# A fused attention and mixture-of-experts layer on one core: the first chunk's front worked in halves of two token tiles

## The chip, the core and the metric

The kernel runs on one core of a Trainium2 chip. The metric is device time in microseconds (us). The engines are TensorE (PE in the profile, its weight loads PEld), VectorE (DVE), ScalarE (ACT), GpSimd (POOL) and SyncE (SP), which issues most DMAs. The kernel before took 575.56 us, the median of three runs (575.51 to 577.62).

## The reference

`x` holds 4096 tokens (2 x 2048) of 256 features. It is normalised (`xn`), and three things are added: `x` itself, an attention branch and a feed-forward branch, both fed by `xn`.

```python
xn = (x - mean(x)) / sqrt(var(x) + eps)
# attention: 16 heads of 16; q, k, v = xn @ W_in.T
xq, xk = clip(q / 4, -1, 1), clip(k / 4, -1, 1)
Tq, Tk = cheb(xq), cheb(xk)                    # Chebyshev polynomials
num = (Tq * cumsum(Tk * v) * beta).sum(orders) # prefix sums over the tokens
den = (Tq.sum(-1) * cumsum(Tk.sum(-1)) * beta).sum(orders)
attn = (num / (den + eps)) @ W_out.T
# feed-forward: a second layernorm, one routed expert of 8, one shared
xf = layernorm(xn) * ln_w + ln_b
top = argmax(xf @ router_w); w = sigmoid(max(xf @ router_w))
routed = (silu(w*xf @ gate[top]) * (w*xf @ up[top])) @ down[top]
shared = (silu(xf @ sh_gate) * (xf @ sh_up)) @ sh_down
out = x + attn + xn + routed + shared
```

Everything is float32.

## The kernel before

The tokens are cut into 8 chunks of 512, and a chunk into NT = 4 tiles of 128 tokens. A bank is one of six 128x512 places for products.

**Front of a chunk** (`stat` L415, `roots` L425, `front` L467). For each tile DVE computes mean and variance (L420, L421). For all tiles of a group (chunk 0 alone, chunk 1 alone, then 2 and 3, then 4 to 7) `roots` adds epsilon (L432, L433), ACT takes square roots (L435), DVE inverts and refines them (L440 to L444) and forms the bias and scale columns `nm` (L449 to L451). `front` normalises the tiles to `z` (L479 on DVE, L483 on ACT), PE transposes them by feature half `k`, four tiles into one bank (L504), and each bank is evicted with `ln_w` and `ln_b` into the transposed operand `xfT` (L507 on ACT, L509 on DVE). In chunk 0 `k` = 0 is evicted by ACT and `k` = 1 by DVE; the statistics of all later chunks wait for chunk 0's DVE eviction (`evicted`). Chunk 0 also gets its attention operand by PE: ACT writes `xn` for each tile (L496), PE transposes it (L524), the copies go to `xnT` (L526, L527). Later chunks get `xnT` by a row of ratios that goes through memory (L461 to L471, L517). L562 turns X into the sum's start, x + xn. `z`, and for later chunks `xnT` and `xfT`, are spilled to memory by SP (L528, L567, L572).

**The rest.** Router logits (L540, L548); `route` (L634) sorts the tokens by expert and makes tables of slots (PE at L699, L700, L817); `shared` (L840) multiplies `xfT` by the gate and up weights in four column blocks `f` (L849, products `pg` and `pu`), takes silu on ACT (L855), multiplies on DVE (L857) and applies the down weights (L866, added to X at L882, for the very last tiles in two steps at L873); `attend` (L888) does the attention of a chunk, whose products start at L911; `expert` (L1081) takes a tile of slots: gather (L1107), transposes (L1115), gate and up (L1125), silu and product (L1131, L1133), transposes (L1138, L1140, L1141), down (L1146), copy (L1149, L1150), scatter to `y_dram` (L1153). At the end `y_dram`, the routed result, is read chunk by chunk (L1175) once all scatters have landed, added to X (L1184) and X is stored (L1188).

**What sets the order.** Each step is recorded as an operation with an engine, a planned cost, what it reads and writes, the buffers it takes and a priority (`op`, L113). `Plan.order` (L156) then walks through planned time: whenever an engine is free, it takes the ready operation of the lowest priority number whose buffers are to be had. What comes out is a fixed order of instructions for each engine; at run time an engine runs its own in that order and waits on semaphores. So a change of one operation's cost, priority or needs can alter the order of the whole program. `shared` products have the highest numbers (`SHA` = 50 and up), so PE takes them where nothing else is ready.

Of the kernel before, what the change touches and what calls it, by code (L numbers as in the profile page):

```python
# [20 lines left out]
P = 128  # L21
# [233 lines left out]
def kernel(  # L255
# [158 lines left out]

    def stat(c):  # L415
        for t in range(NT):
            i = c * NT + t

            def f(c=c, t=t, i=i):
                V.bn_stats(stats[:, i, :], X[c][:, t, :])  # L420
                V.bn_aggr(mv[:, i, :], stats[:, i, :])  # L421

            op("DVE", 0.58, f, r=[("X", c, t)], w=[("mv", i)], prio=FRONT + 0.1 * c - 0.15, after=evicted)

    def roots(cs):  # L425
        a, b = cs[0] * NT, (cs[-1] + 1) * NT
        n = slice(a, b)
        keys = [("mv", i) for i in range(a, b)]
        p = FRONT + 0.1 * cs[0] + 0.01

        def f():
            V.tensor_scalar(ve[:, 0, n], mv[:, n, 1], EPS, None, ALU.add)  # L432
            V.tensor_scalar(ve[:, 1, n], mv[:, n, 1], 1.0 + EPS, EPS * EPS, ALU.mult, ALU.add)  # L433
        op("DVE", 0.35, f, r=keys, w=[("ve", a)], prio=p)
        op("ACT", 0.21, lambda: A.activation(rs[:, :, n], ve[:, :, n], AF.Sqrt),  # L435
           r=[("ve", a)], w=[("rs", a)], prio=p, table="sqrt")

        def h():
            r_, u_, v_ = rs[:, :, n], nu[:, :, n], ve[:, :, n]
            V.reciprocal(r_, r_)  # L440

            V.tensor_tensor(u_, r_, r_, ALU.mult)
            V.scalar_tensor_tensor(u_, u_, -0.5, v_, ALU.mult, ALU.mult)
            V.scalar_tensor_tensor(r_, u_, 1.5, r_, ALU.add, ALU.mult)  # L444
        op("DVE", 0.8, h, r=[("ve", a), ("rs", a)], w=[("r", a // NT + k) for k in range(len(cs))], prio=p)

        def h():

            V.scalar_tensor_tensor(nm[:, 0, n], mv[:, n, 0], -1.0, rs[:, 0, n], ALU.mult, ALU.mult)  # L449
            begun.append(V.tensor_scalar(nm[:, 1, n], rs[:, 0, n], 1.0, None, ALU.add).ins)  # L450
            V.scalar_tensor_tensor(nm[:, 2, n], mv[:, n, 0], -1.0, rs[:, 1, n], ALU.mult, ALU.mult)  # L451

            if a:
                V.tensor_tensor(ratio[:, n], rs[:, 1, n], ve[:, 1, n], ALU.mult)
                V.tensor_tensor(ratio[:, n], ratio[:, n], rs[:, 0, n], ALU.mult)
        op("DVE", 0.8, h, r=[("ve", a)] + [("r", c) for c in cs] + keys,
           w=[("nm", c) for c in cs] + [("ratio", a)], prio=p + 0.015)
        if a:

            pr, row = Buf(bank_p, f"pr_{a}"), Buf(ratio_p, f"row_{a}")  # L460
            op("PE", MT, lambda: T_.transpose(pr.t[: b - a, :P], ratio[:, n], ident), r=[("ratio", a)], w=[pr],  # L461
               alloc=[pr, row], prio=p - 0.5)
            op("ACT", 0.25, lambda: A.copy(row.t[: b - a, :P], pr.t[: b - a, :P]), r=[pr], w=[row], prio=p - 0.5)
            op("POOL", 1.0, lambda: G.dma_start(out=ratio_dram[a:b], in_=row.t[: b - a, :P]),
               r=[row], w=[("ratio_dram", c) for c in cs], nbytes=8 * KiB, prio=p)

    def front(c):  # L467
# [7 lines left out]
        for t in range(NT):  # L475
            i = c * NT + t

            def f(t=t, i=i):
                V.tensor_scalar(zall[:, i, :], X[c][:, t, :], mv[:, i, 0:1], rs[:, 1, i : i + 1],  # L479
                                ALU.subtract, ALU.mult)  # L480

            def f_(t=t, i=i):
                A.activation(zall[:, i, :], X[c][:, t, :], AF.Identity,  # L483
                             bias=nm[:, 2, i : i + 1], scale=rs[:, 1, i : i + 1])
            if c:
                op("ACT", 0.59, f_, r=[("X", c, t), ("r", c), ("nm", c)], w=[("z", i)], prio=p, alt=[("DVE", 0.36, f)])
            else:
                op("DVE", 0.36, f, r=[("X", c, t), ("r", c)], w=[("z", i)], prio=p)
        xnT, xfT = Buf(xnT_p, f"xnT_{c}"), Buf(xfT_p, f"xfT_{c}")
        v2 = lambda b: b.t.rearrange("p (k t) -> p k t", k=KD)  # L490
        if c == 0:

            xn2 = [Buf(ratio_p, f"xn_{i}") for i in range(2)]
            v4 = lambda t: xn2[t // 2].t[:, ts(t % 2, D)]
            for t in range(NT):
                op("ACT", 0.59, lambda t=t: A.activation(  # L496
                    v4(t), X[0][:, t, :], AF.Identity, bias=nm[:, 0, t : t + 1], scale=rs[:, 0, t : t + 1]),
                   r=[("X", 0, t), ("nm", 0)], w=[(xn2[t // 2], t)], prio=p, alloc=[xn2[t // 2]] if t % 2 == 0 else [])
        for k in range(KD):
            bk = Buf(bank_p, f"tr_{c}_{k}")  # L500

            def f(bk=bk, k=k):
                for t in range(NT):
                    T_.transpose(bk.t[:, ts(t, P)], zall[:, c * NT + t, ts(k, P)], ident)  # L504
            op("PE", 4 * MT, f, r=[("z", c * NT + t) for t in range(NT)] + ([rows] if c else []), w=[bk],
               alloc=[bk, xfT, xnT] if k == 0 else [bk], prio=p)
            on = [("ACT", 0.77, lambda bk=bk, k=k: A.activation(  # L507
                v2(xfT)[:, k, :], bk.t, AF.Identity, bias=lnb[:, k : k + 1], scale=lnw[:, k : k + 1])),
                  ("DVE", 0.69, lambda bk=bk, k=k: V.tensor_scalar(  # L509
                v2(xfT)[:, k, :], bk.t, lnw[:, k : k + 1], lnb[:, k : k + 1], ALU.mult, ALU.add))]  # L510

            o = op(*on[k if c == 0 else 0], r=[bk, "ln"], w=[(xfT, k)],
               prio=p if c else -2.0, alt=on[1:] if c else [])
            if c == 0:
                evicted[:] = [o]
            if c:
                op("DVE", 0.69, lambda bk=bk, k=k: V.tensor_tensor(v2(xnT)[:, k, :], bk.t, rows.t, ALU.mult),  # L517
                   r=[bk, rows], w=[(xnT, k)], prio=p)
        for k in range(KD if c == 0 else 0):
# [10 lines left out]
           r=[("z", c * NT + t) for t in range(NT)], w=[("z_dram", c)], nbytes=512 * KiB, prio=p)  # L530
        fronts.append(xfT)
        if c % 2:
# [4 lines left out]
            def f():  # L537
                for k in range(KD):
                    for i in range(2):
                        T_.matmul(pl.t[ts(i * KD + k, QD), :], rw[:, k, :], v2(pair[i])[:, k, :],  # L540
                                  start=True, stop=True)
            op("PE", 1.0, f, r=[(b, k) for b in pair for k in range(KD)] + ["rw"], w=[pl], alloc=[pl], prio=p)
            lgT = Buf(tv_p, f"lgT_{c}")
# [15 lines left out]
        for t in range(NT):  # L559
            i = c * NT + t  # L560
            kw = dict(bias=nm[:, 0, i : i + 1], scale=nm[:, 1, i : i + 1])
            op("ACT", 0.59, lambda t=t, kw=kw: A.activation(X[c][:, t, :], X[c][:, t, :], AF.Identity, **kw),  # L562
               r=[("nm", c), (xfT, 0)], w=[("X", c, t)], prio=ROUTE + 1.0)
        if c < STAY:
            xfTs[c] = xfT
        else:
            op("SP", 0.45, lambda: S_.dma_start(out=xf_dram[c], in_=v2(xfT)),  # L567
               r=[(xfT, 0), (xfT, 1)], w=[("xf_dram", c)], nbytes=512 * KiB, prio=p)
        if c == 0:
# [5 lines left out]
    for cs in ([0], [1], [2, 3], [4, 5, 6, 7]):  # L575
        for c in cs:
            stat(c)
        roots(cs)
        for c in cs:
# [50 lines left out]

    op("POOL", 6.5, constants, r=[("nm", 0)], w=["constants"], prio=FRONT)


    def route():  # L634
# [36 lines left out]
        def f():  # L671
# [4 lines left out]
            V.tensor_scalar(edge, iota[:, : NJ + 1], float(P), None, ALU.mult)  # L676
        op("DVE", 0.8, f, r=["iota_i"], w=["iota", "tok1"] + ones_hot + whats, alloc=ones_hot + whats, prio=FRONT + 0.75)
        op("DVE", 0.42, lambda: V.tensor_reduce(top, logits, AX.X, ALU.max),
# [155 lines left out]
    def load_T(kind, c, pool, src, prio, gate):  # L834
        b = Buf(pool, f"{kind}_{c}")
        op("SP", 0.45, lambda: S_.dma_start(out=b.t.rearrange("p (k t) -> p k t", k=KD), in_=src[c]),
           r=[(f"{kind}_dram", c)], w=[(b, 0), (b, 1)], alloc=[b], nbytes=512 * KiB, prio=prio, after=gate)
        return b

    def shared(c, gate):  # L840
# [3 lines left out]
        for f in range(KF):  # L844
            pg, pu, h = Buf(bank_p, f"pg_{c}_{f}"), Buf(bank_p, f"pu_{c}_{f}"), Buf(hT_p, f"hT_{c}_{f}")

            def mm(b, wt, f=f):
                for k in range(KD):
                    T_.matmul(b.t, wt[:, k, ts(f, P)], vx(k), start=(k == 0), stop=(k == KD - 1))  # L849
            o = op("PE", 2 * MM, lambda mm=mm, pg=pg: mm(pg, sg), r=[(xfT, 0), (xfT, 1), "sg"], w=[pg],  # L850
                   alloc=[pg, pu, h], prio=SHA + c)
            first = first or o
            op("PE", 2 * MM, lambda mm=mm, pu=pu: mm(pu, su), r=[(xfT, 0), (xfT, 1), "su", pg], w=[pu],
               prio=SHA + c - 0.1)
            op("ACT", 0.62, lambda h=h, pg=pg: A.activation(h.t, pg.t, AF.Silu), r=[pg], w=[h], prio=SHQ,  # L855
               table="silu")
            op("DVE", 0.69, lambda h=h, pu=pu: V.tensor_tensor(h.t, h.t, pu.t, ALU.mult), r=[pu, h], w=[h],  # L857
               prio=SHQ)
            hT.append(h)
# [371 lines left out]
```

## Time and profile before

| | |
|---|---|
| median of 3 runs | 575.56 us (575.51, 575.56, 577.62) |
| the profiled execution | 576.52 us, of which the span from first to last instruction is 574.5 |
| first instruction of PE | 7.85 us after the span's start |
| end of PE's last product | 570.80 |
| DVE busy, 100 to 200, 200 to 300, 300 to 400, 400 to 500 | 94.3, 94.2, 93.0, 91.8 us |
| bytes moved by DMA | 132.67 MB, mean 231 GB/s |

In the timeline a row gives the start, the length, engine, line, operation, what is written and read, and a count where equal instructions are merged; a bracket says how long the engine was idle before and what ended that. A float32 product or transpose that the program has once can appear as two records (512 columns), or as one (a transpose). Matmuls overlap, so the time of one in a row of many is the distance between starts, not the length of a record.

### The profile page before, as it was taken

How to read it: one execution, taken by the hardware profiler on the slowest of the kernel's cores; microseconds unless marked ns; L12 is line 12 of the kernel's file. 1: busy time of each engine (PE TensorE's matmuls, PEld its weight loads, DVE VectorE, ACT ScalarE, POOL GpSimd, SP SyncE). 2: the span in 40 equal slices, each digit the busy share in tenths (PEclk: the TensorE clock that was granted, in tenths of full speed). 3: DMA queues.
4: the chain of work that ended last, by engine and by line, in shares of the span. 5: the costliest groups of instructions: out<-in, count | busy, mean ns of one | idle time of the engine just before them, and what ended most of it. 6: DMA issues, size and time to landing. Idle time of an engine off the chain costs nothing.

```text
span 574.5 us, 8088 instructions
## 1 busy us (share of the span) xinstructions
PE 562.9 (98%) x2651; PEld 303.7 (53%) x2651; DVE 485.0 (84%) x787; ACT 240.4 (42%) x471; POOL 95.1 (17%) x113
## 2 busy tenths in 40 slices
PE   4999999999999999999999999999999999999997
PEld 2456564765554644564664545545454555653565
DVE  5989999998999999899999999999998999721353
ACT  5679973014532553363355445435442632221100
POOL 4111000022033011203212030221222112010100
PEclk9999999999999999999999999999999999999999
DMA  8857660644369739817994995799398679950395
GB/s 283 269 163 254 224 254 2 240 159 134 110 222 376 233 91 352 289 65 218 317 342 154 294 317 207 238 373 373 93 323 277 201 243 371 375 199 10 102 309 183
DMA packets 87689, 132.67 MB, mean 231 GB/s; under 512 B 5681, under 2 KB 52063, under 8 KB 87648
## 3 DMA queue, kind: packets, MB, share of 16 engines
q1 hardware_dynamic: 83152, 121.65, 63.1%
q0 software_dynamic: 3952, 10.51, 5.4%
q8 instruction: 21, 0.34, 0.3%
q14 instruction: 20, 0.16, 0.1%
q10 hardware_dynamic: 544, 0.00, 0.1%
HBM read 113.26 MB, written 19.15 MB: 230 GB/s over the span
## 4 chain that ended last, share of the span: by engine, by line
PE 98%; DVE 1%; DMA 0%; issue 0%; DVEq 0%
PE bank L1125 22%; PE bank L849 20%; PE bank L911 15%; PE bank L1146 11%; PE bank L866 10%; PE bank L1049 5%; PE bank L1138 3%; PE psk L941 3%; PE psq L941 2%; PE bank L504 1%; PE bank L1115 1%; PE bank L817 1%; PE psk L954 1%; PE psk L1035 1%; PE bank L540 1%; PE bank L1022 0%
## 5 line engine op out<-in xcount | busy, mean ns | idle before, releaser
L1125 PE MATMUL bank<-big,wide 128*32 128x512 f32 (+1 forms) x360 | 106.2, 596 | 0.0
L1153 POOL DMA_INDIRECT y_dram<-wide,give_i x33 | 41.9, 1270 | 308.7 <-ACT wide L1149 140.1
L911 PE MATMUL bank<-xnT,w_in 128*128 128x512 f32 x192 | 86.3, 595 | 0.0
L978 DVE TENSOR_TENSOR_SCAN tv<-ones,carry,tv 128x512 f32<-128x512 f32 x60 | 76.7, 1278 | 1.1
L849 PE MATMUL bank<-xfT,sg 128*128 128x512 f32 x128 | 62.8, 614 | 0.0
L1125 PEld LDWEIGHTS bank<-big,wide 128*32 128x32 f32 (+1 forms) x360 | 37.1, 147 | 46.5 <-issue 42.5
L849 PE MATMUL bank<-xfT,su 128*128 128x512 f32 x128 | 60.6, 595 | 0.0
L866 PE MATMUL bank<-sd,hT 128*128 128x256 f32 x256 | 57.5, 380 | 0.0
L911 PEld LDWEIGHTS bank<-xnT,w_in 128*128 128x128 f32 x192 | 35.7, 190 | 39.1 <-issue 36.5
L855 ACT ACTIVATE hT<-bank 128x512 f32<-128x512 f32 x32 | 19.1, 597 | 84.5 <-PE bank L849 83.5
L866 PEld LDWEIGHTS bank<-sd,hT 128*128 128x128 f32 x256 | 48.0, 190 | 10.0 <-issue 3.5
L1107 POOL DMA_INDIRECT wide<-z_dram,take_i x33 | 37.6, 1141 | 84.9 <-DVE give_i L828 68.4
L1146 PE MATMUL bank<-big,wide 128*32 128x256 f32 (+1 forms) x312 | 48.5, 384 | 0.0
L998 DVE TENSOR_TENSOR o<-o,tv 128x512 f32<-128x512 f32 x64 | 44.4, 694 | 1.8
L1131 ACT ACTIVATE wide<-bank,slot_s 128x512 f32<-128x512 f32 x33 | 22.7, 687 | 50.0 <-PE bank L1125 50.0
L1146 PEld LDWEIGHTS bank<-big,wide 128*32 128x32 f32 (+1 forms) x312 | 32.0, 144 | 18.7 <-issue 10.1
L849 PEld LDWEIGHTS bank<-xfT,sg 128*128 128x128 f32 x128 | 23.5, 194 | 29.0 <-issue 26.8
L933 DVE SCALAR_TENSOR_TENSOR T<-T 128x1024 f32<-128x1024 f32 x32 | 38.0, 1215 | 0.0
L849 PEld LDWEIGHTS bank<-xfT,su 128*128 128x128 f32 x128 | 23.5, 190 | 26.4 <-issue 25.5
L1133 DVE SCALAR_TENSOR_TENSOR wide<-bank,slot_s,wide 128x512 f32<-128x512 f32 x33 | 24.7, 747 | 13.6 <-PE bank L1125 12.4
L857 DVE TENSOR_TENSOR hT<-hT,bank 128x512 f32<-128x512 f32 x32 | 21.8, 682 | 16.3 <-PE bank L849 15.8
L919 ACT ACTIVATE T<-bank 128x512 f32<-128x512 f32 x32 | 19.1, 597 | 39.4 <-PE bank L911 39.4
(206 smaller groups left out, 884.2 us busy)
## 6 DMA issues: line engine op xcount, KB each, us to landing
big<-in_gate_w SPq DMA_DIRECT2D x46, 512.0 KB, 6.0
big<-in_up_w SPq DMA_DIRECT2D x44, 512.0 KB, 4.8
big<-in_down_w SPq DMA_DIRECT2D x39, 512.0 KB, 7.4
xfT<-in_down_w SPq DMA_DIRECT2D x15, 512.0 KB, 7.3
xfT<-in_up_w SPq DMA_DIRECT2D x9, 512.0 KB
z_dram<-big SPq DMA_DIRECT2D x8, 512.0 KB, 6.3
xfT<-in_gate_w SPq DMA_DIRECT2D x8, 512.0 KB, 5.7
X<-in_x SPq DMA_DIRECT2D x7, 512.0 KB
```

The lines of the kernel that those rows point to most:

```text
L849: T_.matmul(b.t, wt[:, k, ts(f, P)], vx(k), start=(k == 0), stop=(k == KD - 1))
L866: T_.matmul(po.t[:, ts(i, D)], hT[f].t[:, ts(tp * 2 + i, P)], sd[:, f, :], start=(f == 0), stop=(f == KF - 1))
L911: T_.matmul(pm.t, w_in[:, k, ds(i * D + g * P, P)], xnT.t[:, ts(k, CH)], start=(k == 0), stop=(k == KD - 1))
L933: op("DVE", 1.27, lambda i=i, j=j, q=part: V.scalar_tensor_tensor(q[i](), q[j](), off[i], q[1](), ALU.subtract, ALU.mult), r=[(T, j)] + X2 ...
L941: T_.matmul(pt.t[ts(i - 1, QD), :], heads[:, 24 - g * HB : 24 - g * HB + QD], half[i](side), start=(g == 0), stop=(g == KD - 1 and (i > KD ...
L978: o_ = op("DVE", 1.25, lambda b=b, i=i, g=g: V.tensor_tensor_scan(b.t, ones[:, 0:1].to_broadcast([P, CH]), b.t, 0.0 if opening else old[:, ...
L998: op("DVE", 0.66, lambda o=o, b=b: V.tensor_tensor(o(), o(), b.t, ALU.add), r=[b, ok], w=[ok], prio=p)
L1049: T_.matmul(pa.t[:, ts(i, D)], o2.t[:, ds(g * CH + (tp * 2 + i) * P, P)], w_out[:, g, :], start=(g == 0), stop=(g == KD - 1))
L1107: op("POOL", 1.28, lambda: G.indirect_dma_start(out=zt.t, out_offset=None, in_=z_dram, in_offset=bass.IndirectOffsetOnAxis(ap=take_i[:, j ...
L1125: T_.matmul(b.t[n, :], xT.t[:, ds(k * P + n.start, n.stop - n.start)], wt.t[:, ts(k, FF)], start=(k == 0), stop=(k == KD - 1), skip_group_ ...
L1146: T_.matmul(py.t[n, :D], hmT.t[:, ds(i * P + n.start, n.stop - n.start)], wd.t[:, ts(i, D)], start=(i == 0), stop=(i == KF - 1), skip_grou ...
L1153: y_ins.append(G.indirect_dma_start(out=y_dram, out_offset=bass.IndirectOffsetOnAxis(ap=give_i[:, j : j + 1], axis=0), in_=yt.t, in_offset ...
```

## The change

Chunk 0 goes through the front in two halves of two tiles.

- **Statistics and roots.** The first three tiles' statistics come first; the fourth tile's wait for the first half's inverse roots. `roots` runs for tiles 0 and 1, then for tiles 2 and 3. The columns `nm` are split off into `means`, which for chunk 0 runs once for all four tiles and waits for the first half's DVE eviction.
- **Transposes and evictions.** A bank now holds both feature halves of two tiles. Each half is evicted by two instructions of 128x256, `k` = 0 on ACT and `k` = 1 on DVE.
- **Products.** For `f` = 0 and 1 of chunk 0 gate and up products are issued by halves of 256 columns with priorities of their own (-5, -4.5, -4, -3.5); silu and the DVE product follow once for both halves.
- **Waits.** The casts of `route` (L672 to L676) and the statistics of later chunks wait for the last half's DVE eviction. GpSimd's `constants` (L584) waits for `nm` as before. Evictions of later chunks get the priority -2.0.

```diff
+    HT = NT // 2
+    def part(c, t):
+        return (0, t // HT) if c == 0 else (c, 0)
+    def xf_keys(c, b, h=None):
+        return [(b, k, n) for k in range(KD) for n in ((0, 1) if c == 0 else (0,)) if h in (None, n)]
...
-        op("DVE", 0.8, h, r=[("ve", a), ("rs", a)], w=[("r", a // NT + k) for k in range(len(cs))], prio=p)
+        scaled = op("DVE", 0.8, h, r=[("ve", a), ("rs", a)], w=[("r", k) for k in parts], prio=p)
+        return parts, p, scaled
+    def means(a, b, parts, p, behind=()):
...
+        for h in range(2 if c == 0 else 0):
+            bk = Buf(bank_p, f"tr_{c}_{h}")
+            hs = slice(h * HT * P, (h + 1) * HT * P)
+            for t in range(h * HT, (h + 1) * HT):
+                def f(bk=bk, h=h, t=t):
+                    for k in range(KD):
+                        T_.transpose(bk.t[:, ds((k * HT + t - h * HT) * P, P)], zall[:, t, ts(k, P)], ident)
+                op("PE", 2 * MT, f, r=[("z", t)], w=[(bk, t)],
+                   alloc=[] if t % HT else [bk, xfT, xnT] if h == 0 else [bk], prio=-6.0)
...
+            op("ACT", 0.46, lambda src=src, hs=hs: A.activation(
+                v2(xfT)[:, 0, hs], src(0), AF.Identity, bias=lnb[:, 0:1], scale=lnw[:, 0:1]),
+               r=keys, w=[(xfT, 0, h)], prio=-2.0)
+            o = op("DVE", 0.42, lambda src=src, hs=hs: V.tensor_scalar(
+                v2(xfT)[:, 1, hs], src(1), lnw[:, 1:2], lnb[:, 1:2], ALU.mult, ALU.add),
+               r=keys, w=[(xfT, 1, h)], prio=-2.0)
+            if h == 0:
+                means(0, NT, [(0, 0), (0, 1)], FRONT, [o])
+            evicted[:] = [o]
...
+        if cs == [0]:
+            stat(0, range(HT + 1))
+            stat(0, range(HT + 1, NT), [roots(0, HT)[2]])
+            roots(HT, NT)
...
-        op("DVE", 0.8, f, r=["iota_i"], w=["iota", "tok1"] + ones_hot + whats, alloc=ones_hot + whats, prio=FRONT + 0.75)
+        op("DVE", 0.8, f, r=["iota_i"], w=["iota", "tok1"] + ones_hot + whats, alloc=ones_hot + whats, prio=FRONT + 0.75, after=evicted)
...
+            halves = (0, 1) if c == 0 and f < 2 else (None,)
+            for n in halves:
+                def mm(b, wt, f=f, n=n):
+                    cols = slice(0, CH) if n is None else slice(n * CH // 2, (n + 1) * CH // 2)
+                    for k in range(KD):
+                        T_.matmul(b.t[:, cols], wt[:, k, ts(f, P)], vx(k)[:, cols], start=(k == 0), stop=(k == KD - 1))
+                cost, q = (2 * MM, SHA + c) if n is None else (2 * M256, -5 + n)
+                o = op("PE", cost, lambda mm=mm, pg=pg: mm(pg, sg), r=xf_keys(c, xfT, n) + ["sg"], w=[(pg, n)],
+                       alloc=[] if n else [pg, pu, h], prio=q)
+                first = first or o
+                op("PE", cost, lambda mm=mm, pu=pu: mm(pu, su), r=xf_keys(c, xfT, n) + ["su", (pg, n)], w=[(pu, n)],
+                   prio=q - 0.1 if n is None else q + 0.5)
```

## The prediction

> **What bounds the kernel now.** I read the page's busy shares and its chain of waits first, then what TensorE waited for, then the timelines of the first 36 us and of the last 45.
>
> ```profile
> PE 562.9 (98%) x2651; PEld 303.7 (53%) x2651; DVE 485.0 (84%) x787; ACT 240.4 (42%) x471; POOL 95.1 (17%) x113
> ...
> PE 98%; DVE 1%; DMA 0%; issue 0%; DVEq 0%
> ...
> PE bank L504 <- DVE big L479: 7.9, 1, 7.9
> ```
>
> TensorE (PE) carries the chain, and its list of waits has one entry: 7.9 us before its first instruction. From then on it is never short of work. So the time is the sum of three parts: what lies ahead of dense PE work, the PE work itself (which the order hardly alters), and what lies behind its last product. The change acts on the first part; the planner, which orders the whole program anew, may act on the last.
>
> The front, from the timelines:
>
> ```profile
> 5.66 0.17 DVE L432 TENSOR_SCALAR ve<-mv 128x4 f32<-128x4 f32 x1
> ...
> 5.93 0.21 ACT L435 ACTIVATE rs<-ve 128x8 f32<-128x8 f32 x1 [2.61 <-DVE ve L433]
> ...
> 6.46 0.20 DVE L440 RECIPROCAL rs<-rs 128x8 f32<-128x8 f32 x1
> ...
> 7.29 1.38 DVE L479 TENSOR_SCALAR big<-X,mv,rs 128x256 f32<-128x256 f32 x4
> ...
> 9.29 0.76 ACT L507 ACTIVATE xfT<-bank,lnb,lnw 128x512 f32<-128x512 f32 x1
> ```
> ```profile
> 7.85 2.20 PE L504 MATMUL bank<-ident,big 128*128 128x128 f32 x8 [7.85 <-DVE big L479]
> 10.10 3.78 PE L849 MATMUL bank<-xfT,sg 128*128 128x512 f32 x4
> 13.68 1.29 PE L524 MATMUL bank<-ident,wide 128*128 128x128 f32 x8
> 14.80 1.88 PE L849 MATMUL bank<-xfT,su 128*128 128x512 f32 x4
> ```
>
> The reader is to see two things. PE's first product waits for the eviction that ends at 10.05. And the four records from 10.10 take 3.58 us to the next instruction, those from 14.80 only 1.72 (the next starts at 16.52): 0.85 us against 0.43 apiece. PE runs at half rate until about 14.2, where the pitch of the L524 transposes halves; the PEclk column says 1.00 all the same.
>
> The end:
>
> ```profile
> 536.33 0.98 POOL L1153 DMA_INDIRECT y_dram<-wide,give_i  x1 [1.87 <-DMA y_dram<-wide,give_i]
> ...
> 538.96 0.92 SPq L1175 DMA_DIRECT2D xnT<-y_dram  x2
> ...
> 567.38 0.69 DVE L882 TENSOR_TENSOR X<-X,bank 128x512 f32<-128x512 f32 x1 [1.44 <-PE bank L866]
> 568.11 1.22 DVE L1184 TENSOR_TENSOR X<-X,xfT 128x1024 f32<-128x1024 f32 x1
> 570.84 0.75 DVE L873 TENSOR_TENSOR X<-X,bank 128x256 f32<-128x256 f32 x2 [1.51 <-PE bank L866]
> ```
>
> PE ends at 570.80. The whole add of the routed result (L1184) is done before; only two 128x256 adds and their stores follow. The span ends at 574.47, 3.67 us behind PE.
>
> **The front, step by step.** Two tiles' statistics need two pairs at a pitch of 0.53 (the pairs start at 3.39, 3.95, 4.48): the second aggregate starts at 4.38, the added epsilon 0.22 later as in before (5.44 to 5.66), Sqrt at 4.87 (0.20 behind the second of them). The third tile's pair fills VectorE (DVE) until 5.27; Reciprocal stands there, the first normalised tile 0.83 later (6.46 to 7.29) at 6.10, the second at 6.43, the first transpose 0.56 behind the first (7.29 to 7.85): 6.66. The half's last transpose starts near 7.3 and ends near 7.7. ScalarE (ACT) must run the second half's Sqrt first, which its queue holds ahead of the eviction: the fourth tile's pair starts at 6.76, so Sqrt runs 7.68 to 7.89. The 128x256 eviction isn't in the trace; between 0.46 (L1118, 128x128) and 0.77 (L507, 128x512) I take 0.56: it ends at 8.40, and the first product starts at 8.45 instead of 10.10, 1.65 us sooner.
>
> From there nothing leaves PE idle: two gate ops of four 256-column records (1.71 each at half rate) last to 11.9, the second half's transposes, whose tiles are normalised by 9.8, to 12.8, and two up ops on the first half cover the second half's evictions, done near 13.5. Moved work: the means, the casts and the next statistics stand later on DVE, under those ops; the xn copies start near 9.9 and are done near 15, PE transposes them near 19. SyncE's (SP) loads keep their order: gate and up weights are issued at 2.69 and 3.17, and at the 300 GB/s of the first 20 us the 1.05 MB up to the gate weights are in by about 7; the cover is 1 us, and a later landing would shift the first product one for one.
>
> Work done by 14.2, in full-rate time, with a transpose at 0.109 (eight from 33.91 to 34.78): before, eight transposes (0.87) and half of the 3.9 us since 10.10 (1.96), together 2.83; after, four transposes (0.44) and half of the 5.7 us since 8.45 (2.87, the other four among it), together 3.31. Gain **0.47**, if full rate comes at the same time. If it moves forward by the same 1.65, half of that more: **1.30**. One trace can't tell what sets the moment of full rate, so both ends: 4.1 us later (the dense stretch ahead of it, 10.1 to 14.2) turns the 0.47 into a loss of 1.6, as much sooner into a gain of 2.5. I take 0.9, between the two readings.
>
> [...]
>
> **PE work.** Sixteen 512-column records become 32 of 256: 0.216 each (3.46 us for 16, L866) against 0.429 (5.15 for 12, L911), +0.05. In the built order PE changes between full and quarter-array products 131 times instead of 128; a change costs 0.09 (0.52 against 0.43 ahead of L941): +0.28. Elsewhere products that wait for an ACT or DVE step stand at least 1.1 us of PE work behind its source, against 1.0 before: no new stall, at 0; bounds 0 and 3, a few such waits of under a microsecond each behind a DVE that is 92 to 94% busy from 100 to 500.
>
> **The tail.** Six of chunk 0's eight gate and up ops now stand before the first attention product, instead of three, and everything from there on stands later in PE's order. Behind the last expert's product the built order holds 8 gate/up ops and 32 down products, 13.7 + 13.8 = 27.5 us; in before it is 36.3 (534.5 to 570.8). The scatter, and with it the loading of the routed result, comes 8 us nearer to PE's end: first load about 24 us before it, not 31.8.
>
> On DVE the closing rows are now: the add of X7's first half, a 128x256 add, X5's routed add, a 128x256 add, X7's routed add. The first 128x256 add waits for PE's very last product, as in before (570.84 behind 570.80). So behind PE's end E: add at E+0.04; X5 at +0.37; second add at +1.5; X7 at +1.96 for 1.22, to **+3.18** (before +0.79). Then three stores instead of the last one, 0.44 apart, the last issued at +4.2; from the last issue (571.73) to the span's end are 2.74: **E+6.94**, against 3.67: **+3.27**. Both loads have landed by then: X7's waits for X3's add near E-5 and needs under 4 us (563.92 to 567.88). Bounds: +2.0 if the adds overlap better, +5 if the loads run late, since 8.4 MB of loads and stores then share 24 us instead of 32.
>
> Sum: -0.9 + 0.05 + 0.28 + 3.27 = **+2.7**. The profiled execution took 576.52 (span 574.5), so 579.2 against its own; it lies 0.96 above the median of 575.56. Of the four times shown (575.51, 575.56, 576.52, 577.62) the middle is 576.04, which gives **578.7**.
>
> **Rivals.** (A) the forecast, 578.7, its own range 577.8 to 580.2; chance 0.48. [...] Chance 0.39. (C) Starved PE: a full DVE queue holds a step that PE needs, or late loads stretch the tail; +2 to +3: 581 to 582. PE's empty list of waits speaks against it; chance 0.10. (D) The tail stays as it was and only the front counts, 576.0 - 0.6 = 575.4; the built order on DVE speaks against it; 0.03. Faster by 0.5% would need 572.7, which none reaches.
>
> Half a percent is about what a measurement of this kernel can tell from no change; that is 578.4. Slower: A above it 0.43, and C 0.10: 0.53. Faster: 0.02. Same: 0.45. The range leaves out a tenth on each side: 576.2 to 581.2.
>
> **What would show it.** PE's first transpose near 6.7 and first product near 8.5, its waits otherwise none; X7's routed add as the last DVE instruction, starting about 2 us behind PE's end; span end 7 us behind PE's end. Wrong if PE's list of waits holds entries past 10 us, if PE ends much off 570.2, or if the closing adds stand otherwise.

## The result and the profile after

The changed kernel takes **579.5 us** (median of 8 runs, 578.38 to 579.76), the kernel before 576.25 in the same comparison (8 runs, 575.51 to 578.19): ratio 1.0048, 95% interval 1.0035 to 1.0061 (the quotient of the two medians is 1.0056). Beside the later runs the kernel before was run 101 more times: median 576.75, median span 574.8.

The page's busy times and its chain:

```profile
PE 561.9 (97%) x2667; PEld 305.6 (53%) x2667; DVE 488.4 (85%) x797; ACT 239.6 (42%) x470; POOL 91.9 (16%) x113
...
PE 97%; DVE 1%; DMA 0%; issue 0%; ACT 0%
```

PE's list of waits (engine, what it waited with, what it waited for, total, times, longest):

```profile
PE bank L517 <- DVE big L497: 6.7, 1, 6.7
PE bank L893 <- ACT xfT L522: 1.2, 1, 1.2
```

PE still carries the chain, and both of its waits lie in the first 9 us. The time around PE's work is where to look. The front, from the timelines of PE, DVE and ACT:

```profile
6.67 1.09 PE L517 MATMUL bank<-ident,big 128*128 128x128 f32 x4 [6.67 <-DVE big L497]
7.80 0.54 DVE L525 TENSOR_SCALAR xfT<-bank,lnw,lnb 128x256 f32<-128x256 f32 x1
8.38 0.56 ACT L522 ACTIVATE xfT<-bank,lnb,lnw 128x256 f32<-128x256 f32 x1 [0.46 <-DVE xfT L525]
8.99 3.71 PE L893 MATMUL bank<-xfT,sg 128*128 128x256 f32 x8 [1.24 <-ACT xfT L522]
12.54 0.60 PE L517 MATMUL bank<-ident,big 128*128 128x128 f32 x4
12.98 1.89 PE L893 MATMUL bank<-xfT,su 128*128 128x256 f32 x8
```

Read the bracket of the third row: ACT's eviction waited for DVE's, although the two write different halves of `xfT`. Eight records from 8.99 take 3.55 us to the next instruction, eight from 12.98 take 1.73 (the next starts at 14.71): PE reaches full rate at 12.5 here, at 14.2 in before.

The end, on GpSimd, SP and DVE:

```profile
542.99 0.98 POOL L1198 DMA_INDIRECT y_dram<-wide,give_i  x1 [8.25 <-DVE wide L1195]
...
546.60 0.37 SPq L1220 DMA_DIRECT2D xnT<-y_dram  x1
...
565.33 0.45 SPq L1220 DMA_DIRECT2D xfT<-y_dram  x1
...
566.38 0.69 DVE L927 TENSOR_TENSOR X<-X,bank 128x512 f32<-128x512 f32 x1 [0.42 <-PE bank L911]
...
569.83 0.42 DVE L918 TENSOR_TENSOR X<-X,bank 128x256 f32<-128x256 f32 x1 [2.77 <-PE bank L911]
570.17 1.22 DVE L1229 TENSOR_TENSOR X<-X,xfT 128x1024 f32<-128x1024 f32 x1
571.31 0.42 DVE L918 TENSOR_TENSOR X<-X,bank 128x256 f32<-128x256 f32 x1
571.76 1.23 DVE L1229 TENSOR_TENSOR X<-X,xfT 128x1024 f32<-128x1024 f32 x1
```

PE ends at 569.80 (E), 1.00 sooner than in before. DVE's last add, X7's routed one, ends 3.19 behind E, and the span at 576.9, 7.1 behind E, where it was 3.67. So in these two executions: 1.0 us won ahead of E, 3.4 lost behind it.

### The profile page after: what moved, and what is told of

The parts are those of the page before. It is cut to its first block, busy times and chain, and to the rows that moved or that the text cites. A ratio compares the mean times of both kernels' runs of the same rounds, so it can differ in the third digit from the quotient of the medians.

```text
span 576.9 us, 8132 instructions
## 1 busy us (share of the span) xinstructions
PE 561.9 (97%) x2667; PEld 305.6 (53%) x2667; DVE 488.4 (85%) x797; ACT 239.6 (42%) x470; POOL 91.9 (16%) x113
## 4 chain that ended last, share of the span: by engine, by line
PE 97%; DVE 1%; DMA 0%; issue 0%; ACT 0%
PE bank L1170 22%; PE bank L893 20%; PE bank L956 14%; PE bank L1191 11%; PE bank L911 10%; PE bank L1094 5%; PE psk L986 3%; PE bank L1183 3%; PE psq L986 2%; PE bank L1160 2%; PE bank L857 1%; PE bank L544 1%; PE psk L999 1%; PE psk L1080 1%; PE bank L574 1%; PE bank L1067 0%
## 5 line engine op out<-in xcount | busy, mean ns | idle before, releaser
L1170 PE MATMUL bank<-big,wide 128*32 128x512 f32 (+1 forms) x372 | 110.1, 597 | 0.0
L1198 POOL DMA_INDIRECT y_dram<-wide,give_i x33 | 38.9, 1179 | 310.1 <-ACT wide L1194 178.4
L1170 PEld LDWEIGHTS bank<-big,wide 128*32 128x32 f32 (+1 forms) x372 | 37.5, 146 | 51.1 <-issue 47.8
L893 PE MATMUL bank<-xfT,sg 128*128 128x512 f32 (+1 forms) x136 | 62.3, 585 | 1.2 <-ACT xfT L522 1.2
L893 PE MATMUL bank<-xfT,su 128*128 128x512 f32 (+1 forms) x136 | 60.8, 571 | 0.0
L1191 PE MATMUL bank<-big,wide 128*32 128x256 f32 (+1 forms) x312 | 50.0, 385 | 0.0
L1191 PEld LDWEIGHTS bank<-big,wide 128*32 128x32 f32 (+1 forms) x312 | 34.2, 148 | 15.1 <-issue 8.5
L893 PEld LDWEIGHTS bank<-xfT,sg 128*128 128x128 f32 x136 | 25.8, 198 | 25.8 <-issue 21.5
L893 PEld LDWEIGHTS bank<-xfT,su 128*128 128x128 f32 x136 | 24.8, 190 | 26.0 <-issue 24.4
L1170 PE MATMUL bank<-xfT,wide 128*32 128x512 f32 (+1 forms) x76 | 36.2, 599 | 0.0
L1029 ACT COPY carry<-tv 128x1 f32<-128x1 f32 x80 | 15.2, 189 | 46.9 <-DVE tv L1023 45.6
```

The costliest lines, as they stand in the source:

```text
L893: T_.matmul(b.t[:, cols], wt[:, k, ts(f, P)], vx(k)[:, cols], start=(k == 0), stop=(k == KD - 1))
L1170: T_.matmul(b.t[n, :], xT.t[:, ds(k * P + n.start, n.stop - n.start)], wt.t[:, ts(k, FF)], start=(k == 0), stop=(k == KD - 1), skip_group_ ...
L1191: T_.matmul(py.t[n, :D], hmT.t[:, ds(i * P + n.start, n.stop - n.start)], wd.t[:, ts(i, D)], start=(i == 0), stop=(i == KF - 1), skip_grou ...
L1198: y_ins.append(G.indirect_dma_start(out=y_dram, out_offset=bass.IndirectOffsetOnAxis(ap=give_i[:, j : j + 1], axis=0), in_=yt.t, in_offset ...
```

## The experiments

Theory: the changed order of the closing adds keeps the end, and the front gives a part of it back. Rivals: late loads of the routed result keep the end, by their bytes or by their late issue; the moved products cost by themselves; the front gives nothing. Below, "tail" is the time from E to the span's end in the profiled execution.

**1. The adds moved back** (`tail_early`: X5's and X7's routed adds ahead of the two closing 128x256 adds).

```diff
-    for _, _, emit in plan.order():
+    made = plan.order()
...
+    for c in (5, 7):
+        made.insert(at_(tails[0]), made.pop(at_(adds[c])))
+    for _, _, emit in made:
         emit()
```

> The changed kernel with one thing moved: the routed adds of chunks 5 and 7 stand ahead of the two closing 128x256 adds on VectorE; every other engine's order is the same. Theory (the loss is the closing order): X7's load was issued at 565.33 and needs about 4 us (563.92 to 567.88 in the kernel before), so X7's add runs 569.3 to 570.5 and the closing adds end near 571.2, from which 2.9 us remain: span 574.1 in place of 576.9, time 579.5 - 2.8 = 576.7, PE's start and end unchanged. Rival 1 (the late loads and stores set the end by their bytes): the adds only wait for their data in another order, 578.5 or more. Rival 2 (the loss lies in the front or on PE): 579.5 as it is.

Measured: 578.39 (ratio to before 1.0033, 1.0022 to 1.0044), tail 6.6. Only 1.1 of the expected 2.8 us came back, and the interval overlaps with the changed kernel's; in the profiles the tail is 0.6 shorter and E the same. DVE's timeline:

```profile
567.04 1.23 DVE L1230 TENSOR_TENSOR X<-X,xfT 128x1024 f32<-128x1024 f32 x1
571.23 1.23 DVE L1230 TENSOR_TENSOR X<-X,xfT 128x1024 f32<-128x1024 f32 x1 [2.97 <-DMA xfT<-y_dram]
572.56 0.75 DVE L919 TENSOR_TENSOR X<-X,bank 128x256 f32<-128x256 f32 x2
```

DVE now waits 2.97 us for X7's load, issued at 565.33 and landed at 571.14. The DMA engines are full then; by stretches (busy time and count of PE, PEld, DVE, ACT and POOL, granted clock, DMA share, GB/s):

```profile
555.00:560.00 5.00, 5.00 (x13) 2.28 (x12) 1.78 (x3) 0.60 (x1) 0.00 (x0) 1.00 1.01 326
560.00:565.00 5.00, 5.00 (x18) 3.15 (x17) 3.39 (x5) 0.60 (x1) 0.00 (x0) 1.00 0.96 318
565.00:570.00 5.00, 4.80 (x23) 3.88 (x21) 2.84 (x3) 0.00 (x0) 0.00 (x0) 1.00 0.99 285
```

**2. The changed closing order put into before** (`before_late`).

```diff
+    m = made.pop(at_(adds[5]))
+    made.insert(at_(tails[0]) + 1, m)
+    m = made.pop(at_(adds[7]))
+    made.insert(at_(tails[1]) + 1, m)
+    m = made.pop(at_(outs[5, 0]))
+    made.insert(at_(adds[5]) + 1, m)
+    for t in (3, 2, 0):
+        m = made.pop(at_(outs[7, t]))
+        made.insert(at_(adds[7]) + 1, m)
```

> The kernel before with the changed kernel's closing order: on VectorE first half add, X5's routed add, second half add, X7's routed add, and the stores of both chunks behind them; loads, PE and ACT as they were. Theory (the closing order alone is the price): 3.2 us behind PE's end in place of 0.8, and three stores behind it, +3.3: 576.25 + 3.3 = 579.5. Rival (the price comes from the late loads, which this kernel does not have): no more than +1, 577.2.

Measured: 580.72 (1.0063, 1.0047 to 1.0079), tail 7.1, with the DMA engines at a share of 0.32 from 565 to 570. Its DVE rows are those of the changed kernel, with no wait for a load among them:

```profile
571.75 0.42 DVE L874 TENSOR_TENSOR X<-X,bank 128x256 f32<-128x256 f32 x1 [2.76 <-PE bank L867]
572.09 1.22 DVE L1185 TENSOR_TENSOR X<-X,xfT 128x1024 f32<-128x1024 f32 x1
573.22 0.41 DVE L874 TENSOR_TENSOR X<-X,bank 128x256 f32<-128x256 f32 x1
573.67 1.23 DVE L1185 TENSOR_TENSOR X<-X,xfT 128x1024 f32<-128x1024 f32 x1
```

The order alone is enough for the tail. The time is 4.1 above before, not 3.4. In this profile the front is late as well (first transpose at 9.33, PE's end at 571.71), because DVE waits for the load of the fourth tile of `x`:

```profile
6.45 0.43 DVE L421 BATCH_NORM_STATS2 stats<-X 128x6 f32<-128x256 f32 x1 [1.35 <-DMA X<-in_x]
```

Whether it was so in all six runs isn't known.

**3 and 4. A quarter of the closing bytes left out** (`cut`: no stores of chunks 0 to 3; `cut_early`: in addition the edit of run 1).

```diff
+    for c in (0, 1, 2, 3):
+        for t in range(NT):
+            if (c, t) in outs:
+                made.pop(at_(outs[c, t]))
```

> The changed kernel without the stores of chunks 0 to 3 (2.1 of the 8.4 MB of closing loads and stores; those outputs are left out), every other instruction in the same order, the closing adds still in the changed order. Theory, two causes that overlap, each enough by itself: the order of the adds alone keeps the tail, DVE's last add ends 3.2 us behind PE's end, the span 7 us behind it, 579 us, as the changed kernel. Rival, late loads alone make the tail: with a quarter of the bytes gone it shrinks to some 4 us behind PE's end, 576.3 us.

> The same with the routed adds of X5 and X7 ahead of the two closing adds as well, so both suspects are gone. Theory: X7's load lands before PE's end, the adds that wait for PE's last product are again the last of DVE, the span ends 3.7 us behind PE's end, 575.5 us (575 to 576.3). Rival, something else in the tail (the last store's landing, the loads' own latency): as with the adds moved alone, 578.4 us.

Measured: `cut` 579.39 (1.0052, 1.0035 to 1.0070), tail 7.3: nothing gained, although the DMA share from 560 to 565 fell from 0.95 to 0.43. With the order as changed, these bytes don't matter. `cut_early` 577.28 (1.0016, 1.0005 to 1.0027), tail 5.3: with both gone 2.2 us of the changed kernel's 579.5 come back, but not the expected 4.0. Its DVE rows say what is left:

```profile
563.45 1.22 DVE L1230 TENSOR_TENSOR X<-X,xfT 128x1024 f32<-128x1024 f32 x1
...
569.56 1.22 DVE L1230 TENSOR_TENSOR X<-X,xfT 128x1024 f32<-128x1024 f32 x1 [1.51 <-DMA xfT<-y_dram]
570.89 0.75 DVE L919 TENSOR_TENSOR X<-X,bank 128x256 f32<-128x256 f32 x2
```

X7's load takes the buffer of X3's, so it is issued when X3's add (563.45) is done, at 564.69, and needs 4.8 us even with the engines half idle before it.

**5 and 6. X7's load issued sooner** (`tail_fix`: run 1 with X7's add ahead of X5's, X3's add one DVE step earlier, X7's load ahead of X5's load and X3's store in SP's queue; `cut_fix`: the same without the stores of chunks 0 to 3).

```diff
+    for c in (7, 5):
+        made.insert(at_(tails[0]), made.pop(at_(adds[c])))
+    made.insert(at_(adds[4]) + 1, made.pop(at_(adds[3])))
+    made.insert(at_(loads[5]), made.pop(at_(loads[7])))
+    made.insert(at_(loads[5]) + 1, made.pop(at_(outs[3, 0])))
```

> The changed kernel, all work done, with the routed adds of X7 and X5 ahead of the two closing adds (as in the run that moved the adds alone), and in addition X3's routed add directly behind X4's (one DVE product earlier) and X7's load ahead of X5's load and X3's store in SP's queue. X7's load is then issued near 562.5 instead of 565.3. Theory, the late load of X7 is late because it is issued late: it lands near 567, both adds are done by about 570.2, the span ends some 4.2 us behind PE's end, 576.5 us (576 to 577.2). Rival, the DMA engines are full and the bytes decide: the loads land no sooner, 578.4 us.

> The order with X7's early load, and without the stores of chunks 0 to 3 (those outputs are left out): the closing order, the late issue of X7's load and the full DMA engines are all gone, with PE's order and the front as in the changed kernel. Theory: these three are the whole price of the tail; X7's load is issued near 562.3 and lands by 567, the two closing adds start right behind PE's last product, the span ends 3.7 us behind it, 575.3 us. Rival, the short time between the last scatter and PE's end costs something beyond these: the span ends over 4.5 us behind PE's end, 576.5 us or more.

Measured: `tail_fix` 578.60 (1.0038, 1.0025 to 1.0050), tail 6.2, no better than run 1. The time is the rival's, but not for the rival's reason, that the loads land no sooner:

```profile
567.82 2.57 DVE L1230 TENSOR_TENSOR X<-X,xfT 128x1024 f32<-128x1024 f32 x2 [0.87 <-DMA xfT<-y_dram]
570.31 0.74 DVE L919 TENSOR_TENSOR X<-X,bank 128x256 f32<-128x256 f32 x2
```

X7's load is issued at 562.44, its add runs at 567.82, 3.4 us sooner than in run 1, and both routed adds are done by 570.39, nearly as the theory had it (E is 569.68). What is late is the stores behind them: the last is issued at 572.47, 2.8 us behind E, where it is 0.9 in before, and from there 3.4 us remain, against 2.74. The DMA engines are full (share 1.00 and 321 GB/s from 560 to 565).

`cut_fix` 577.97 (1.0026, 1.0015 to 1.0038), tail 5.4, no better than `cut_early`. Here the rival holds, something beyond the three costs time:

```profile
567.79 2.42 DVE L1230 TENSOR_TENSOR X<-X,xfT 128x1024 f32<-128x1024 f32 x2
570.52 0.75 DVE L919 TENSOR_TENSOR X<-X,bank 128x256 f32<-128x256 f32 x2 [0.32 <-PE bank L912]
```

The closing adds wait for PE again (570.52, E is 570.48), as in before, and yet the tail is 1.8 longer. X5's add, second of the two, ends at 570.21, so X5's store is issued at 570.23 and X7's first one at 570.65, right ahead of the last two (571.20 and 572.29); in before X5's store goes at 565.97 and X7's first at 569.36. The last issue is 0.9 later behind E and the span's end 0.9 later behind the last issue (3.6 against 2.74). How much of the latter is the stores' queueing wasn't separated.

**7. The moved products alone** (`before_prio`: before, with chunk 0's `f` = 0 and 1 at the priorities -5 and -4.5, whole).

```diff
-                   alloc=[pg, pu, h], prio=SHA + c)
+                   alloc=[pg, pu, h], prio=-5 if c == 0 and f < 2 else SHA + c)
...
-               prio=SHA + c - 0.1)
+               prio=-4.5 if c == 0 and f < 2 else SHA + c - 0.1)
```

> The kernel before with one part of the change: chunk 0's first four gate and up products (f = 0 and 1, whole, not by halves) get the priorities -5 and -4.5. Six gate and up products then stand ahead of the first attention product, as in the changed kernel, but 32.7 us of PE work stay behind the last expert product and the closing adds keep the order of before. Theory: the moved work costs nothing by itself, 576.5 us (576 to 577). Rival, shared work moved ahead lengthens the program wherever the closing adds stand: 578 us or more.

Measured: 576.97 (1.0005, 0.9992 to 1.0018), tail 3.7. Its last scatter is issued at 540.15, 32.0 us ahead of E, against 26.8 in the changed kernel and 34.5 in before. So the moved products cost nothing by themselves; here the planner kept the closing order of before, and the closing phase stayed some 5 us longer than the changed kernel's.

**8. Two banks for a half** (`banks`: each half's transposes go to two banks, one per feature half).

```diff
-            bk = Buf(bank_p, f"tr_{c}_{h}")
+            bk = [Buf(bank_p, f"tr_{c}_{h}_{k}") for k in range(KD)]
```

> The changed kernel with each half's transposes in two banks, one for each feature half, so that ScalarE and VectorE evict from different banks; the order on every engine is the same. Theory (the shared bank makes the second eviction wait for the first, 8.38 behind 8.34): ACT's eviction starts behind its Sqrt, near 7.95, the first product near 8.55 in place of 8.99, worth 0.2 to 0.45: 579.1 to 579.3. Rival (ACT waits for the lnw and lnb loads or its queue): eviction at 8.38 and first product at 8.99 as they are.

Measured: 578.67 (1.0033, 1.0023 to 1.0044), span 0.9 below the changed kernel's (576.95 against 577.85, medians).

```profile
7.75 0.54 DVE L525 TENSOR_SCALAR xfT<-bank,lnw,lnb 128x256 f32<-128x256 f32 x1
7.77 0.55 ACT L522 ACTIVATE xfT<-bank,lnb,lnw 128x256 f32<-128x256 f32 x1
...
8.37 3.78 PE L893 MATMUL bank<-xfT,sg 128*128 128x256 f32 x8 [0.66 <-ACT xfT L522]
```

The evictions run side by side and the first product starts 0.62 sooner: the shared bank was what ACT waited for. PE ends at 569.41, 0.4 sooner, the upper end of the 0.2 to 0.45 that were expected; the 0.8 us between the medians of the times are more than that, and the moment of full rate (12.2 here) differs between executions.

**9 and 10. PE busy ahead of the front** (`warm`: eleven identity products, with no reader, ahead of the changed kernel's first transpose; `best`: these, two banks and the moved adds together).

```diff
+    for _ in range(11):
+        T_.matmul(psq_p.places[0][:, :P], ident, ident, start=True, stop=True)
```

> The changed kernel with eleven 128x128 products of the identity with itself at PE's very start, into a bank that is not in use then; their result is read by nothing. Theory (full rate follows dense PE work, wherever it comes from): the products that took 0.427 a record until 12.5 take 0.216 from 8.99 on, half of 3.5 us is won: 577.7, and the second half's transposes stand near 10.7. Rival (the moment of full rate is set by something else than PE's own work, or is lost in the pause until 8.99): the pitch stays 0.427 until 12 or so, 579.5.

> The changed kernel with three edits together: two banks for each half's transposes, the routed adds ahead of the two closing adds, eleven identity products ahead of PE's first transpose. Theory: PE ends near 567.9, the late loads still hold the end near 6.6 us behind that, span 574.5, 576.2 us: no better than the kernel before. If the edits add up (1.0, 0.8 and 2.3 us below 579.4): 575.3 us.

Measured: `warm` 577.02 (1.0013, 1.0001 to 1.0026), PE's end 568.21, 1.6 sooner. `best` 576.34 (1.0001, 0.9986 to 1.0015), as fast as before; but in its profile PE ends only at 569.44. The two timelines and, for each, the clock from 8 to 12:

```profile
1.44 5.06 PE L1238 MATMUL psq<-ident 128*128 128x128 f32 x22 [1.44 <-POOL ident masks.py:199]
6.50 0.82 PE L517 MATMUL bank<-ident,big 128*128 128x128 f32 x4
8.69 1.99 PE L893 MATMUL bank<-xfT,sg 128*128 128x256 f32 x8 [1.37 <-ACT xfT L522]
```
```profile
8.00:12.00 4.00, 3.31 (x17) 2.96 (x18) 2.40 (x12) 1.92 (x4) 1.82 (x13) 1.00 1.06 387
```
```profile
1.44 4.46 PE L1243 MATMUL psq<-ident 128*128 128x128 f32 x22 [1.44 <-POOL ident masks.py:199]
6.59 0.76 PE L518 MATMUL bank<-ident,big 128*128 128x128 f32 x4 [0.69 <-DVE big L498]
8.43 3.68 PE L894 MATMUL bank<-xfT,sg 128*128 128x256 f32 x8 [1.08 <-ACT xfT L523]
```
```profile
8.00:12.00 4.00, 3.57 (x9) 2.76 (x10) 1.66 (x10) 1.47 (x3) 1.76 (x12) 0.57 1.06 388
```

In the first (`warm`) eight half products take 1.83 us to the next start, full rate; in the second (`best`) 3.51, half rate, and the clock column says it: 0.57. In this execution full rate was granted near 5.1 (the distance of the identity products halves from 0.21 to 0.11) and is gone at the first product, behind the two pauses that the brackets show. The times of both kernels lie in two groups with nothing between (`warm` eight at 576.63 to 577.20 and four at 578.12 to 578.90; `best` seven to 576.36 and five from 577.65), 1.8 to 2.0 us apart, about what 3.5 us at half rate cost; the one profile of each fits its group. So does the mean clock of the executions: 0.993 or 0.994 in the four slower ones of `warm` and in four of the five of `best`, 0.996 to 0.999 in the others.

**11. All edits and a filled pause** (`fill`: run 5, two banks, thirteen identity products ahead, six between the first half's transposes and the first product).

> All edits together on the changed kernel: the order of the previous run, two banks for each half's transposes, thirteen identity products ahead of PE's first transpose and six between the first half's transposes and the first product (nothing left out). Theory: PE is busy from 1.4 us on without a pause over 0.7 us, so that it is at full rate from the first product in every execution; PE ends near 567.7, the span 4.2 us later, 573.8 us, faster than the kernel before (576.7). Rival, the pause is not what brings half rate back: in a third of the executions the time is 1.8 us longer, as in the two earlier runs with such products.

Measured: 575.87 (0.9983, 0.9971 to 0.9995), 575.06 to 576.85 without two groups, which speaks for the pause as what brings half rate back. In its profile full rate comes at 7.4, PE has no pause from 1.44 to the first product, and that product starts at 9.05, later than in run 10, because the added products are in its way. The tail is 5.8, not 4.2, much as in run 5 (6.2): that is 1.6 of the 2.1 us that are missing.

**12. The busy PE alone, on before** (`before_warm`: eighteen identity products ahead of its first transpose).

> The kernel before with eighteen identity products ahead of PE's first transpose, otherwise unchanged. Theory: half rate from 10.1 to 14.2 is gone and the eight transposes run at full rate, 2.0 to 2.6 us sooner, 574.3 us, as much as all that the halves could give. Rival, a program whose first product stands later keeps half rate for a while after the eviction's pause: 576 us.

Measured: **575.06** (0.9970, 0.9960 to 0.9981), 574.36 to 575.24, the fastest of all, between the theory's 574.3 and the rival's 576; in the profile PE ends at 568.75, 2.05 sooner, as the theory had it. Its front:

```profile
1.44 5.74 PE L1193 MATMUL psq<-ident 128*128 128x128 f32 x36 [1.44 <-POOL ident masks.py:199]
7.81 1.74 PE L504 MATMUL bank<-ident,big 128*128 128x128 f32 x8 [0.64 <-DVE big L479]
10.15 1.98 PE L849 MATMUL bank<-xfT,sg 128*128 128x512 f32 x4 [0.60 <-ACT xfT L507]
11.97 1.04 PE L524 MATMUL bank<-ident,wide 128*128 128x128 f32 x8
```

The four records from 10.15 take 1.82 us instead of 3.58, and the tail stays at 3.7. The first product isn't sooner at all. What the halves were to win by an earlier start lies in PE's rate, and it is to be had without touching the order.

## Why the prediction was right, and where its steps were not

**The sum** was +2.7, and against all 101 later runs of before it is 579.5 - 576.75 = +2.75 (+3.25 in the comparison of eight runs each). By medians of the spans it is made of: +3.05 in the span (577.85 against 574.8), of which the tail, read from one profile each, is +3.47 and the rest, -0.4, what PE won; and -0.3 around the span (579.5 less 577.85 is 1.65; before it is 1.95), which the prediction took as equal. So the forecast (A) came, and the closing order that it named is enough for the tail by itself (run 2). That the sum fits to a tenth is luck: the tail was put 0.2 too low, PE's work 0.3 and the time around the span 0.3 too high, and the front's gain, by the medians, 0.5 too large.

**The first product** was put at 8.45 and came at 8.99. The first transpose (6.66, measured 6.67) and the length of the eviction (0.56, measured 0.56) were right. The step that failed is the start of ACT's eviction, put right behind its Sqrt at 7.84 (8.40 less 0.56): the change puts both feature halves into one bank, and ACT then runs behind DVE's 0.54. In before each had a bank of its own; run 8 gave that back and got 0.62. The rows 7.80 and 8.38 show one eviction behind the other, those of run 8 (7.75 and 7.77) the two side by side.

**Full rate** was left open between two readings. The value between them, 0.9 (0.57 with the added PE work), lies between the 0.4 of the medians and the 1.00 of the profiles. In the profiled execution full rate came at 12.5, 1.7 sooner than in before (14.2). By the prediction's own count, half of that added to the 0.47, this gives 0.47 + 0.85, and the late eviction takes 0.27 of it, half of its 0.54, which leaves the 1.0 that was measured. The rival that had 0.39, not slower because full rate comes sooner, failed all the same: 1.0 us won ahead of E stand against 3.4 lost behind it. And 12.5 is one execution's: the six profiles with this front show 12.2 to 13.9, so there is no single moment to forecast, and a value that fits one execution is luck.

**PE work and stalls.** The +0.33 for the smaller records and the changes between products isn't seen. Count four or eight transposes at 0.109, half of the time from the first gate product to full rate and all of the time from there to E, and PE's work is 559.5 us in both profiles. No wait of PE behind the first product, as said. **C** and **D** didn't come: no starved PE, and the tail did grow. One half of C, the late loads, is there all the same, hidden behind the closing order.

**The tail** was +3.27 and is +3.47; the order of the rows on DVE, their distances (last add to E+3.18, measured 3.19) and the first load (24 us ahead of E, measured 23.2) came as worked out. What the prediction had too simple is why. It counted the order alone, and said that both loads have landed by then, X7's in "under 4 us". Run 1 shows 5.8, landing at E+1.3. Behind the order stands a second cause of almost the same size, from the same 8 us by which the closing phase is shorter: 8.4 MB at the 320 GB/s of run 1 (326 and 318) are an estimated 26 us, and 23.2 are left from the first load to E. The order alone makes the whole tail (runs 2 and 3); the loads alone, with the order put back, still make 2.9 us of it (run 1, 6.6 against 3.7). Removing one gives 0.1 or 1.1, both 2.2 (runs 3, 1, 4). The last 1.7 us did not go with the late load either (run 6): then it is X5's add and store that come late. With the order put back, the price goes with the length of the closing phase: none at 32.0 us from last scatter to E (run 7), 2.5 to 2.9 at 26.8 (runs 5 and 1); nothing between was measured. With the changed order it is paid at 34.5 us too (run 2).

## What to carry to other kernels

When a priority moves work to the front of a packed engine, look at what that work used to cover at the end: here 8 us of products had been hiding the loads, adds and stores of the last phase. Where an order and a transfer are late for one reason, undoing either shows little; undo both before one of them is cleared. And ahead of an engine that starts at half rate, cheap early work of its own may be worth more than an earlier first product (here PE's end came 2.05 us sooner with it, run 12, and 1.00 with the change).

## What the runs showed of the hardware

- **How long half rate lasts varies from execution to execution.** From PE's first gate or identity product (transposes ahead of it left out) to full rate: 3.1 us (`before_late`, `before_warm`), 3.2 (`before_prio`), 3.3 (`cut_early`), 3.5 (changed, `tail_fix`), 3.7 (`best`, `cut`, `tail_early`), 3.8 (`banks`), 4.1 (before), 5.0 (`cut_fix`), 5.4 (`warm`), 6.0 (`fill`).
- **From full rate to the fall of the clock behind PE's end the profiles show two lengths.** The clock column falls to 0.50 behind PE's end, in before at 573.97, 3.17 behind E, in the changed kernel at 572.29, 2.49 behind. From the moment of full rate (in `best` the second, 11.94) to there it is 559.8 us in eleven profiles, these two among them, and 566.6 in the other three (`warm`, `fill`, `before_warm`). So the two moments move together, and neither stands at a fixed distance from PE's own work. What sets them isn't shown.
- **The scatter of before is smaller with the early products:** 575.17 to 578.64 in the 26 runs of before beside run 12, 574.36 to 575.24 in the 11 of run 12. Two things that differ between the profiles may be its sources, the moment of full rate and the start of PE. In the profiles of runs 2 and 7, which have the front of before, the first transpose comes at 9.33 and 8.89 in place of 7.85; in run 2 DVE waits 1.35 us for a tile of `x`. How much each contributes wasn't separated.
- **Full rate was lost behind pauses of about 1 us in one profile and kept behind a longer one in another.** In `best` it is gone behind two of them, 0.69 and 1.08 by the brackets, with four transposes between (half rate from 8.52 to 11.94, clock 0.57 from 8 to 12); behind one of 1.37 in `warm` it is not (1.00), nor behind two of 0.64 and 0.60 in `before_warm` (1.00). So in these rows the longest pause alone doesn't decide it.
- **The clock column shows a rate that was taken back, not one that wasn't granted yet:** 0.57 in `best`, but 1.00 from 8 to 12 in the changed kernel, whose products run at half rate there (eight records in 3.55 us, against 1.73 from 12.98).
- **A 512 KB load of the last phase, X7's, took 5.8 us from issue to landing** in run 1, whose DMA engines are full (share 0.99 from 565 to 570). It took 4.8 in run 4, with them half idle before it (0.46 from 560 to 565), and 4.0 (563.92 to 567.88) in before, at 0.72 and 0.64 in the same two stretches. So how full the engines are doesn't settle it alone.
